# Token rows summed inside the gathering DMAs, into six accumulators, instead of on VectorE

## The chip, the cores and the metric

The kernel runs on one core of one Trainium2 chip. The metric is the device time of one execution in microseconds (us). The times before are 7422.84, 7378.67 and 7359.8 us in three runs, with a median of 7378.67 us. Engines are named as in the profile: PE is TensorE, DVE is VectorE, ACT is ScalarE, POOL is GpSimd and SP is SyncE.

## The reference, cut to what matters

A recommendation model scores 16384 examples. Each example averages 32 rows of a word table (50000 x 300, fp32), averages 20 rows of each of three 64-wide tables, looks up one row in each of four small tables, and sends the 748 numbers through three dense layers. A "wide" sum of scalars is added before the sigmoid.

```python
tok = word_emb[token_idx].mean(axis=1)          # 16384 x 32 rows of 300
e1 = emb_mh1[mh1_idx].mean(axis=1)              # e2, e3 alike; o1..o4 are one row each
emb = jnp.concatenate([tok, e1, e2, e3, o1, o2, o3, o4], axis=1)
h = jax.nn.relu(emb @ W1 + b1)                  # 748 -> 1024, then 512, then 256
...
return jax.nn.sigmoid(h @ Wd + bd + wide)
```

The change concerns `tok` alone: how the 32 rows of an example are fetched and added up.

## The kernel before, in words

The batch is cut into 128 tiles of 128 examples, one example per partition, and four tiles make a block of 512 for the dense layers. For each tile there are four kinds of work.

**Tokens** (`tokens`, L180). Eight groups of four indirect DMAs, issued from POOL (L186), each fetch one 1200-byte row for each of the 128 examples into a quarter of a tile `tok_rows` of 4 x 300 fp32. `tok_rows` has three buffers. DVE then adds the four rows of the group (L194: 600 elements, L197 or L199: 300) and adds them to the example's row `g` (L200). `g` also holds the sums of the small tables and is what the dense layers read.

**Counts** (`one_hots` L255, `counts` L273 and L280). The lookups in the small tables become matrix products. DVE compares the keys of six rows with an iota into two one-hot tiles, `row` and `slice`, which have two buffers. PE multiplies them into a PSUM tile `pc`, twelve matmuls in two groups of six, and ACT evicts each group into `cnt` (L280). A tile takes eleven such steps (`STEPS`), 22 evictions.

**Sums** (`small_sums`, L298 and L305). PE multiplies the counts of the tile before by the tables held in SBUF (138 matmuls `pg`), and DVE reduces the result into `g`.

**Dense layers** (`transposed` L340 and L341, `layer` L348 and L357, `mlp`). They run for the block of four tiles before, in fp32, spread over the steps of the next four tiles.

The order of every engine's queue is the order in which the Python loop at L411 to L445 emits the instructions. There is no scheduler. In step `i` of a tile it emits: the one-hots of step `i+1`, the count matmuls and evictions of step `i`, one portion of the tokens, one portion of the sums, and one portion of the dense layers. `Paced` doles out the portions: the token generator is advanced eight times over the eleven steps, at steps 0, 1, 2, 4, 5, 6, 8 and 9. So a group's three DVE additions stand in DVE's queue between the one-hots of two steps. A fresh buffer of `tok_rows` is free when the additions of the group three earlier are done. POOL does nothing else in the loop but issue these gathers, 32 for each tile.

The semaphores behind the gathers are eight lanes taken in turn, so a gather also waits for the gather eight places before it.

Of the kernel before, what the change touches and what calls it, by code (L numbers as in the profile page):

```python
# [8 lines left out]
F32 = mybir.dt.float32  # L9
# [3 lines left out]
U32 = mybir.dt.uint32  # L13
AF = mybir.ActivationFunctionType
ALU = mybir.AluOpType
AX = mybir.AxisListType

P = 128
N_TOK, TOK_D = 32, 300
N_MH, EMB = 20, 64  # L20
ROW = EMB + 1
D1, D2, D3 = 1024, 512, 256
TOK_GROUP = 4
BLOCK = 512
HALF = P // 2
N_SMALL = 3 * N_MH + 4
ONEHOT = 6
STEPS = -(-HALF // ONEHOT)
LULL = 12
# [14 lines left out]
def kernel(  # L44
# [21 lines left out]
    nc = tc.nc  # L66
    B = out.shape[0]
    NSUB = BLOCK // P
    M1, M2, M3 = D1 // P, D2 // P, D3 // P
# [3 lines left out]
    slices, n_h = {}, 0  # L73
    for f in SMALL:
        n = -(-tables[f].shape[0] // P)
# [5 lines left out]
    idxp = ctx.enter_context(tc.tile_pool(name="idx", bufs=2))  # L81
    keyp = ctx.enter_context(tc.tile_pool(name="keys", bufs=1))
    scp = ctx.enter_context(tc.tile_pool(name="sc", bufs=2))
    tokp = ctx.enter_context(tc.tile_pool(name="tok", bufs=3))
    ohp = ctx.enter_context(tc.tile_pool(name="onehot", bufs=2))
    cp = ctx.enter_context(tc.tile_pool(name="counts", bufs=2))
    gp = ctx.enter_context(tc.tile_pool(name="g", bufs=NSUB + 1))
    wp = ctx.enter_context(tc.tile_pool(name="wide", bufs=2 * NSUB))
    xp = ctx.enter_context(tc.tile_pool(name="x", bufs=1))
    op = ctx.enter_context(tc.tile_pool(name="o", bufs=1))  # L90
    ps_h = ctx.enter_context(tc.tile_pool(name="ps_h", bufs=2, space=bass.MemoryType.PSUM))
    ps_c = ctx.enter_context(tc.tile_pool(name="ps_c", bufs=2, space=bass.MemoryType.PSUM))
    ps_g = ctx.enter_context(tc.tile_pool(name="ps_g", bufs=2, space=bass.MemoryType.PSUM))
# [83 lines left out]
    bd_sb = const.tile([1, 1], F32, name="bd_sb")  # L177
    nc.scalar.dma_start(out=bd_sb, in_=bd)

    def tokens(g, it):  # L180

        for q in range(N_TOK // TOK_GROUP):
            rows = tokp.tile([P, TOK_GROUP * TOK_D], F32, name="tok_rows")
            for t in range(TOK_GROUP):
                j = q * TOK_GROUP + t
                nc.gpsimd.indirect_dma_start(  # L186
                    out=rows[:, t * TOK_D : (t + 1) * TOK_D],
                    out_offset=None,
                    in_=word,
                    in_offset=bass.IndirectOffsetOnAxis(ap=it[:, j : j + 1], axis=0),  # L190
                )
            n = TOK_GROUP * TOK_D // 2
            while n > TOK_D:
                nc.vector.tensor_add(rows[:, 0:n], rows[:, 0:n], rows[:, n : 2 * n])  # L194
                n //= 2
            if q == 0:
                nc.vector.tensor_add(g[:, 0:n], rows[:, 0:n], rows[:, n : 2 * n])  # L197
            else:
                nc.vector.tensor_add(rows[:, 0:n], rows[:, 0:n], rows[:, n : 2 * n])  # L199
                nc.vector.tensor_add(g[:, 0:n], g[:, 0:n], rows[:, 0:n])  # L200
            yield 1

    def load_indices(blk):


        b0 = blk * BLOCK
        it = idxp.tile([P, NSUB, N_TOK], I32, name="it")
        nc.sync.dma_start(
            out=it, in_=idx[b0 : b0 + BLOCK, 0:N_TOK].rearrange("(s p) c -> p s c", p=P)
        )  # L210
        ix = keyp.tile([P, NSUB // 2, 2, N_SMALL], I32, name="ix")
        for s in range(NSUB):
            nc.sync.dma_start(
                out=ix[(s % 2) * HALF : (s % 2 + 1) * HALF, s // 2],
                in_=idx[b0 + s * P : b0 + (s + 1) * P, IDX_MH:IDX_COLS].rearrange(
                    "(f p) c -> p f c", p=HALF
                ),
            )
        return it, ix
# [68 lines left out]
    def small_sums(g, cnt):  # L288


        by_slice = cnt.rearrange("l f p h -> l (f p) h")
        for i in (0, 2, 6, 4):
            pair = SMALL[i : i + 2]
            pg = ps_g.tile([P, 2, 3 * ROW], F32, name="pg")
            for j, f in enumerate(pair):
                h0, h1 = slices[f]
                for h in range(h0, h1):
                    nc.tensor.matmul(  # L298
                        pg[:, j, :], by_slice[:, :, h], terms[:, h, :], start=(h == h0), stop=(h == h1 - 1)
                    )  # L300
                    if h < h1 - 1:
                        yield 1
            at = TOK_D + i * ROW
            n = len(pair)
            nc.vector.tensor_reduce(  # L305
                g[:, at : at + n * ROW].rearrange("p (f d) -> p f d", f=n),
                pg[:, 0:n, :].rearrange("p f (c d) -> p f d c", c=3),
                AX.X,
                ALU.add,
            )  # L310
            yield n if i != 6 else n + LULL
# [32 lines left out]
    def layer(dst, weights, bias, src, kks, n_out):  # L344
        for m in range(n_out):
            ph = ps_h.tile([P, BLOCK], F32, name="ph", tag="ph")
            for k, kk in enumerate(kks):
                nc.tensor.matmul(  # L348
                    ph,
                    weights[:kk, k, m * P : (m + 1) * P],  # L350
                    src[:kk, k, :],
                    start=(k == 0),
                    stop=(k == len(kks) - 1),
                )
                if k < len(kks) - 1:
                    yield 1
            nc.scalar.activation(dst[:, m, :], ph, AF.Relu, bias=bias[:, m : m + 1])  # L357
            yield 1

    def mlp(blk, x, wides):  # L360

        h1 = xp.tile([P, M1, BLOCK], F32, name="h1", tag="odd")
        yield from layer(h1, w1_sb, b1_sb, x, chunk_k, M1)
        h2 = xp.tile([P, M2, BLOCK], F32, name="h2", tag="even")
        yield from layer(h2, w2_sb, b2_sb, h1, [P] * M1, M2)
        h3 = xp.tile([P, M3, BLOCK], F32, name="h3", tag="odd")
        yield from layer(h3, w3_sb, b3_sb, h2, [P] * M2, M3)
        po = ps_h.tile([1, BLOCK], F32, name="po", tag="ph")
        for k in range(M3):
            nc.tensor.matmul(po, wd_sb[:, k : k + 1], h3[:, k, :], start=(k == 0), stop=False)  # L370
        for s, wide in enumerate(wides):
            nc.tensor.matmul(  # L372
                po[:, s * P : (s + 1) * P], wide, ident, start=False, stop=(s == NSUB - 1)
            )
        y = op.tile([1, BLOCK], F32, name="y")
        nc.scalar.activation(y, po, AF.Sigmoid, bias=bd_sb)
        nc.sync.dma_start(
            out=out[blk * BLOCK : (blk + 1) * BLOCK, :].rearrange("n o -> o n"), in_=y
        )
        yield M3  # L380
# [23 lines left out]
    tiles = B // P  # L404
    mlp_size = NK * M1 + M1 * M2 + M2 * M3 + M3
    ctx.enter_context(tc.manual_schedule())
    it, ix = load_indices(0)
    sc = lookup_keys(ix)
    hot = one_hots(sc, 0, 0)
    gs, wides, layers, before = [], [], None, None  # L410
    for t in range(tiles + 1):  # L411
        s = t % NSUB
        sums = None
        if before:
            sums = Paced(small_sums(*before), n_h + LULL, STEPS)
        if t < tiles:
            if s == 0 and t:
                it, sc = next_it, next_sc
            g = gp.tile([P, G_COLS], F32, name="g")
            cnt = cp.tile([P, 2, HALF, n_h], FP8, name="cnt", tag="counts")  # L420
            toks = Paced(tokens(g, it[:, s, :].bitcast(U32)), N_TOK // TOK_GROUP, STEPS)
        for i in range(STEPS):
            if t < tiles:
                hot_now = hot
                if s == 1 and i == 0 and t + NSUB < tiles:
                    next_it, ix = load_indices(t // NSUB + 1)
                if s == 2 and i == 0 and t + NSUB < tiles + 1:
                    next_sc = lookup_keys(ix)
                if i < STEPS - 1:
                    hot = one_hots(sc, s, i + 1)  # L430
                elif t + 1 < tiles:
                    hot = one_hots(next_sc if s == NSUB - 1 else sc, (s + 1) % NSUB, 0)
                counts(cnt, hot_now, i)
                toks.go()
            if sums:
                sums.go()
            if layers:
                layers.go()
        if before:
            sums.finish()  # L440
            gs.append(before[0])
            wides.append(wide_term(before[0]))
        before = (g, cnt) if t < tiles else None
        if len(gs) == NSUB:
            if layers:  # L445
                layers.finish()
            layers = Paced(mlp(t // NSUB - 1, transposed(gs), wides), mlp_size, NSUB * STEPS)
            gs, wides = [], []
# [40 lines left out]
```

## Time and profile before

| What | Value |
|---|---|
| median of three runs | 7378.67 us |
| the profiled execution, its own time | 7632.91 us |
| its span, first to last instruction | 7631.1 us |
| mean granted TensorE clock | 0.874 |
| PE busy | 5876.7 us, 77% |
| DVE busy | 3534.9 us, 46% |
| ACT busy | 2659.7 us, 35% |
| POOL busy | 4052.0 us, 53% |
| gathers (L186) | 4096, 989 ns each |
| gather queue q0 | 629.41 MB, 30.0% of the time of 16 DMA engines |

Busy time is what an engine's instructions cover. A matmul's end is modelled, so PE's busy time says what PE was given, not when the results were there. A gather's POOL time is the time of issuing it; its data lands later. The profiled execution takes 254 us more than the median of the runs, so what is summed from the profile is compared with the profile's own time and then scaled.

### The profile page before, as it was taken

To read this page: it belongs to the slowest core of one execution; us is meant where nothing else is said; L and a number is where in the kernel's file an instruction comes from. 1 tells how busy PE (TensorE), PEld (TensorE's weight loads), DVE (VectorE), ACT (ScalarE), POOL (GpSimd) and SP (SyncE) were. 2 spreads that over 40 slices of the span, in tenths; PEclk is the share of its full clock that TensorE was granted. 3 is DMA by queue.
4 is the path that set the end of the run, shared out by engine and by line. 5 is a ranking of instruction groups with operands and counts; after the bars stand their busy time and mean duration, and the time that the engine had idled before them with its cause. 6 is when DMAs were issued, how large, how long until landed. Compare 5 with 4: busy or idle time off the path is not lost.

```text
span 7631.1 us, 100300 instructions
## 1 busy us (share of the span) xinstructions
PE 5876.7 (77%) x40960; PEld 3502.6 (46%) x40960; DVE 3534.9 (46%) x6977; ACT 2659.7 (35%) x3383; POOL 4052.0 (53%) x4103
## 2 busy tenths in 40 slices
PE   2677877877777777787778788787777777777779
PEld 2444444444444444444444444444444444444444
DVE  4544444444444444454444444444444444444442
ACT  4333333333333333333333333333333333333332
POOL 5555555555555555555555555555555555555551
PEclk8788888888888888888888888888888889888889
DMA  4333333333333333333333333333233333333330
GB/s 133 91 87 87 85 90 83 88 83 88 84 84 86 86 85 86 85 83 89 87 85 88 82 89 85 89 86 86 82 86 87 83 83 88 85 86 88 84 85 26
DMA packets 242810, 652.35 MB, mean 85 GB/s; under 512 B 105631, under 2 KB 109471, under 8 KB 242347
## 3 DMA queue, kind: packets, MB, share of 16 engines
q0 software_dynamic: 196608, 629.41, 30.0%
q1 hardware_dynamic: 42738, 10.83, 0.7%
q8 instruction: 320, 5.24, 0.3%
q10 hardware_dynamic: 3001, 5.69, 0.2%
q14 instruction: 143, 1.17, 0.0%
HBM read 645.59 MB, written 0.07 MB: 85 GB/s over the span
## 4 chain that ended last, share of the span: by engine, by line
PE 51%; another core or an unknown queue 23%; ACT 10%; issue 9%; DVE 4%; POOL 3%; DMA 0%; DVEq 0%; SPq 0%; ACTq 0%; POOLq 0%
PE ph L348 22%; PE pg L298 18%; PE pc L273 9%; ACT cnt L280 8%; POOL tok_rows L186 3%; ACT h L357 2%; PE pt L340 1%; DVE x L341 1%; DVE g L305 1%; PE po L370 1%; DVE slice L255 0%; DVE tok_rows L194 0%; PE po L372 0%; DVE tok_rows L199 0%
## 5 line engine op out<-in xcount | busy, mean ns | idle before, releaser
L186 POOL DMA_INDIRECT tok_rows<-in_word_emb_dram,it x4096 | 4051.1, 989 | 3442.7 <-DVE g L200 1363.5
L280 ACT ACTIVATE cnt<-pc 128x828 fp8e3<-128x828 f32 (+1 forms) x2816 | 2235.8, 840 | 3547.7 <-remote 1763.9
L298 PE MATMUL pg<-terms,cnt 128*128 128x195 bf16 x17664 | 2166.4, 274 | 350.9 <-issue 255.2
L255 DVE TENSOR_TENSOR row<-iota,sc 128x768 bf16<-128x768 bf16 (+1 forms) x1408 | 763.5, 542 | 2947.3 <-remote 1625.3
L298 PEld LDWEIGHTS <-cnt 128*128 128x128 fp8e3 x17664 | 1783.4, 147 | 602.7 <-issue 463.6
L273 PE MATMUL pc<-slice,row 64*128 64x138 bf16 x16384 | 874.2, 233 | 1219.9 <-ACT cnt L280 909.0
L273 PEld LDWEIGHTS <-row 64*128 64x128 bf16 x16384 | 566.3, 98 | 2343.3 <-issue 1831.2
L348 PE MATMUL ph<-x,w_sb 128*128 128x512 f32 (+1 forms) x3072 | 1605.6, 650 | 20.4 <-issue 19.9
L348 PE MATMUL ph<-h,w_sb 128*128 128x512 f32 x2560 | 1366.8, 660 | 21.4 <-issue 20.4
L348 PEld LDWEIGHTS ph<-x,w_sb 128*128 128x128 f32 (+1 forms) x3072 | 588.4, 211 | 489.6 <-issue 480.4
L255 DVE TENSOR_TENSOR slice<-iota,sc 128x828 bf16<-128x828 bf16 (+1 forms) x1408 | 805.0, 572 | 0.0
L194 DVE TENSOR_TENSOR tok_rows<-tok_rows 128x600 f32<-128x600 f32 x1024 | 793.7, 775 | 4.9 <-DMA tok_rows<-in_word_emb_dram,it 4.9
L357 ACT ACTIVATE h<-ph,b_sb 128x512 f32<-128x512 f32 x448 | 308.2, 688 | 1220.0 <-remote 507.5
L348 PEld LDWEIGHTS ph<-h,w_sb 128*128 128x128 f32 x2560 | 494.6, 214 | 410.1 <-issue 409.7
L305 DVE TENSOR_REDUCE g<-pg 128x130 f32<-128x390 f32 (+1 forms) x512 | 250.9, 508 | 836.5 <-remote 396.0
L199 DVE TENSOR_TENSOR tok_rows<-tok_rows 128x300 f32<-128x300 f32 x896 | 423.7, 473 | 30.8
L200 DVE TENSOR_TENSOR g<-g,tok_rows 128x300 f32<-128x300 f32 x896 | 421.8, 471 | 30.7
L341 DVE TENSOR_SCALAR x<-pt,scale 128x512 f32<-128x512 f32 (+1 forms) x192 | 139.0, 748 | 103.7 <-PE pt L340 77.7
L340 PE MATMUL pt<-ident,g 128*128 128x128 f32 (+1 forms) x768 | 126.6, 299 | 59.7 <-DVE x L341 59.7
L340 PEld LDWEIGHTS pt<-ident,g 128*128 128x128 f32 (+1 forms) x768 | 87.2, 147 | 98.8 <-DVE x L341 90.0
L280 ACT ACT_TABLE_LOAD x31 | 39.8, 1283 | 137.8 <-PE pc L273 137.7
L238 PE MATMUL pk<-ident_bf,keys 128*128 128x128 bf16 x128 | 22.5, 245 | 75.7 <-DVE keys L234 41.4
(35 smaller groups left out, 463.5 us busy)
## 6 DMA issues: line engine op xcount, KB each, us to landing
tok_rows<-in_word_emb_dram,it POOLq DMA_INDIRECT x4096
ix<-in_idx_dram SPq DMA_DIRECT2D x128, 32.0 KB
w_sb<-in_W_dram ACTq DMA_DIRECT2D x6, 512.0 KB
w_sb<-in_W_dram ACTq DMA_DIRECT2D x1, 2048.0 KB
it<-in_idx_dram SPq DMA_DIRECT2D x32, 64.0 KB
out_dram<-y SPq DMA_DIRECT2D x32, 2.0 KB
raw<-in_mh_dram SPq DMA_DIRECT2D x1, 422.5 KB
w_sb<-in_W_dram ACTq DMA_DIRECT2D x1, 256.0 KB
```

What stands on the lines that cost most here:

```text
L186: nc.gpsimd.indirect_dma_start(out=rows[:, t * TOK_D : (t + 1) * TOK_D], out_offset=None, in_=word, in_offset=bass.IndirectOffsetOnAxis(ap ...
L194: nc.vector.tensor_add(rows[:, 0:n], rows[:, 0:n], rows[:, n : 2 * n])
L199: nc.vector.tensor_add(rows[:, 0:n], rows[:, 0:n], rows[:, n : 2 * n])
L200: nc.vector.tensor_add(g[:, 0:n], g[:, 0:n], rows[:, 0:n])
L255: nc.vector.tensor_tensor(one[:, 0:rows, :].rearrange("p i (n d) -> p i n d", d=2), iota[:, 0:n].rearrange("p (n d) -> p n d", d=2).unsque ...
L273: nc.tensor.matmul(pc[:, f, k * n_h : (k + 1) * n_h], hot[0][half, k0 + k, :], hot[1][half, k0 + k, :], start=True, stop=True,)
L280: nc.scalar.activation(cnt[:, :, b + k0 : b + k0 + n, :].rearrange("l f k h -> l f (k h)"), pc[:, :, 0 : n * n_h], AF.Copy, scale=0.5, sat ...
L298: nc.tensor.matmul(pg[:, j, :], by_slice[:, :, h], terms[:, h, :], start=(h == h0), stop=(h == h1 - 1))
L305: nc.vector.tensor_reduce(g[:, at : at + n * ROW].rearrange("p (f d) -> p f d", f=n), pg[:, 0:n, :].rearrange("p f (c d) -> p f d c", c=3) ...
L340: nc.tensor.transpose(pt[:kk, s * P : (s + 1) * P], chunk(g, k), ident)
L348: nc.tensor.matmul(ph, weights[:kk, k, m * P : (m + 1) * P], src[:kk, k, :], start=(k == 0), stop=(k == len(kks) - 1),)
L357: nc.scalar.activation(dst[:, m, :], ph, AF.Relu, bias=bias[:, m : m + 1])
```

## The change

It does three things.

1. `gather` replaces the DMA half of `tokens`. At the start of a tile it emits all 32 gathers in POOL's queue. The target is one tile `tok_acc` of six rows of 300 fp32, with two buffers. The first six gathers overwrite an accumulator each; the other 26 carry `compute_op=ALU.add`, so that the DMA adds the fetched row to what the accumulator holds. Gather `j` adds to accumulator `j % 6` and, by the listing of the built instructions, waits for gather `j-6`.
2. The DVE half becomes three additions per tile, of 900, 300 and 300 elements, emitted after the eleven steps of the *next* tile, just ahead of that tile's `wide_term`. The first of them waits for the last gathers of its six accumulators. DVE's queue shrinks from 6864 to 4304 listed rows; PE's and ACT's have as many rows as before.
3. The output pool `op` goes away; the sigmoid's row `y` is kept in a third row of `h3`.

The tile of gathers `t` can start when the additions of tile `t-2` are done, which stand at the end of tile `t-1`'s steps.

```diff
+TOK_ACC = 6
-    tokp = ctx.enter_context(tc.tile_pool(name="tok", bufs=3))
+    tokp = ctx.enter_context(tc.tile_pool(name="tok", bufs=2))
-    op = ctx.enter_context(tc.tile_pool(name="o", bufs=1))
-    def tokens(g, it):
...
+    def gather(it):
+        acc = tokp.tile([P, TOK_ACC * TOK_D], F32, name="tok_acc")
+        for j in range(N_TOK):
+            a = j % TOK_ACC
+            nc.gpsimd.indirect_dma_start(
+                out=acc[:, a * TOK_D : (a + 1) * TOK_D],
+                out_offset=None,
+                in_=word,
+                in_offset=bass.IndirectOffsetOnAxis(ap=it[:, j : j + 1], axis=0),
+                compute_op=ALU.bypass if j < TOK_ACC else ALU.add,
+            )
+        return acc
+    def tokens(g, acc):
+        n = TOK_D
+        nc.vector.tensor_add(acc[:, 0 : 3 * n], acc[:, 0 : 3 * n], acc[:, 3 * n : 6 * n])
+        nc.vector.tensor_add(acc[:, 0:n], acc[:, 0:n], acc[:, n : 2 * n])
+        nc.vector.tensor_add(g[:, 0:n], acc[:, 0:n], acc[:, 2 * n : 3 * n])
...
-        h3 = xp.tile([P, M3, BLOCK], F32, name="h3", tag="odd")
+        h3 = xp.tile([P, M3 + 1, BLOCK], F32, name="h3", tag="odd")
...
-        y = op.tile([1, BLOCK], F32, name="y")
+        y = h3[0:1, M3, :]
...
-            toks = Paced(tokens(g, it[:, s, :].bitcast(U32)), N_TOK // TOK_GROUP, STEPS)
+            acc = gather(it[:, s, :].bitcast(U32))
...
-                toks.go()
...
             sums.finish()
+            tokens(before[0], before[2])
             gs.append(before[0])
             wides.append(wide_term(before[0]))
-        before = (g, cnt) if t < tiles else None
+        before = (g, cnt, acc) if t < tiles else None
```

More of the change, by code (lines that the diff above doesn't have):

```diff
@@ L178 @@
     nc.scalar.dma_start(out=bd_sb, in_=bd)
-    def tokens(g, it):
[L182 to L201, printed above, removed]
+    def gather(it):
[15 more added lines that the diff above has]
+        nc.vector.tensor_add(g[:, 0:n], acc[:, 0:n], acc[:, 2 * n : 3 * n])
     def load_indices(blk):
@@ L414 @@
         if before:
-            sums = Paced(small_sums(*before), n_h + LULL, STEPS)
+            sums = Paced(small_sums(*before[:2]), n_h + LULL, STEPS)
         if t < tiles:
```

## The prediction

> **What bounds the kernel now.** I read the page's groups first, then the waits by engine, then equal stretches of the run with and without dense layers, and last the timeline of one stall.
>
> ```profile
> span 7631.1 us, 100300 instructions
> ...
> PE 5876.7 (77%) x40960; PEld 3502.6 (46%) x40960; DVE 3534.9 (46%) x6977; ACT 2659.7 (35%) x3383; POOL 4052.0 (53%) x4103
> ...
> L186 POOL DMA_INDIRECT tok_rows<-in_word_emb_dram,it x4096 | 4051.1, 989 | 3442.7 <-DVE g L200 1363.5
> ```
>
> PE is at 77%, so the first guess is a PE bound. POOL's waits show how it spends a tile:
>
> ```profile
> POOL tok_rows L186 <- DVE g L200: 1363.5, 338, 8.0
> POOL tok_rows L186 <- issue: 1099.4, 3566, 1.6
> POOL tok_rows L186 <- DVE g L197: 911.1, 118, 16.2
> ```
>
> A gather costs 989 ns plus 0.27 us of issue (1099.4 us over 4096), 1.26 us in all, so 32 gathers keep POOL for 40.2 us a tile. For the other 18 us it waits until DVE's additions free a buffer. The stretches by stage come next: two of tiles that have counts and sums but no dense layers, then one that has them.
>
> ```profile
> core 0: us, PE busy (x) PEld busy (x) DVE busy (x) ACT busy (x) POOL busy (x), PEclk, DMA share, GB/s
> 96.00:156.00 60.00, 26.32 (x272) 21.30 (x270) 26.87 (x57) 17.41 (x22) 36.41 (x37) 0.73 0.35 95
> 212.00:264.00 52.00, 28.60 (x266) 22.48 (x266) 25.42 (x52) 17.33 (x23) 30.09 (x30) 0.64 0.33 90
> 318.00:374.00 56.00, 45.95 (x338) 26.48 (x333) 27.91 (x59) 19.57 (x25) 32.73 (x33) 0.88 0.35 94
> ```
>
> Each stretch is about one tile. PE's work rises from 26 to 46 us and the tile stays near 56. From the trace, by the first count matmul of each tile, tiles 1 to 3 took 60.2, 56.6 and 52.0 us and the later ones 58.5 on average. So PE's own work does not set the tile. A step that runs freely takes 3.5 us, and eleven of them with 2 us of transposes and output products make 40.5 us; 18 us of each tile are stalls. The timeline shows what a stall looks like:
>
> ```profile
> 179.38 0.36 PE L273 MATMUL pc<-slice,row 64*128 64x138 bf16 x6 [1.71 <-issue]
> 179.67 0.89 PEld L298 LDWEIGHTS <-cnt 128*128 128x128 fp8e3 x10
> 180.76 0.47 DVE L200 TENSOR_TENSOR g<-g,tok_rows 128x300 f32<-128x300 f32 x1
> 183.16 0.95 POOL L186 DMA_INDIRECT tok_rows<-in_word_emb_dram,it  x1 [0.30 <-issue]
> ...
> 186.91 0.95 POOL L186 DMA_INDIRECT tok_rows<-in_word_emb_dram,it  x1 [0.30 <-issue]
> 188.48 0.87 ACT L280 ACTIVATE cnt<-pc 128x828 fp8e3<-128x828 f32 x1 [9.15 <-remote]
> 189.40 0.53 PE L273 MATMUL pc<-slice,row 64*128 64x138 bf16 x6 [6.32 <-ACT cnt L280]
> 189.94 0.56 DVE L255 TENSOR_TENSOR row<-iota,sc 128x768 bf16<-128x768 bf16 x1 [8.70 <-PE pc L273]
> ```
>
> The count matmuls were given to PE by 179.5, yet ACT could evict them only from 188.48. Nothing runs from 183 to 188 but POOL's gathers. The release comes when the run of gathers has ended (187.86) and its last data can have landed. I counted evictions over the whole trace by where they fall in a run of gathers (pauses over 1 us end a run), from 264 us on:
>
> - first 6 us of a run: 0.450 a us (19.5 us a tile);
> - the rest of a run: 0.189 a us (21.0 us a tile);
> - the 2.2 us after a run: 0.448 a us (7.0 us a tile);
> - the rest of the pause: 0.553 a us (11.1 us a tile). Free speed is two per 3.5 us, 0.57.
>
> So what shows is that **PE's results come late once gathers have run for 6 us, and recover when they pause**. I infer that the gathers do this; the page shows only that both go together. Runs end by themselves at 4, 8 or 12 gathers, since three buffers hold twelve.
>
> **What the Trainium skill says.** "DMA: Bandwidth & Descriptors", section "SWDGE vs HWDGE vs iDMA": accumulation in a DMA is available only from GpSimd's queue, so all 32 gathers stay on POOL. The same page, "Rules for kernel authors": an accumulating DMA reads its destination and writes it later, so an earlier one on the same bytes must be waited for; the listing of the changed kernel has that wait, on gather j-6. No run here shows its price yet. "SBUF — State Buffer", section "Who interferes with whom": DMA never contends with a compute engine. The counts above do not fit that as they stand, and I go by the counts. "TensorE: Matmul & The Clock Gate", Part 1: the array clock halves when the array is little used. The trace agrees in direction: 0.64 to 0.73 without dense layers, 0.88 with.
>
> **The change part by part**, for one tile.
>
> 1. *DVE's additions.* Removed: L194 793.7, L197 60.2, L199 423.7, L200 421.8, in all 1699.4 us, 13.3 us a tile. Added: 300 elements take 0.47 and 600 take 0.775, so 900 take about 1.08; with two of 0.47, 2.0 us. DVE falls from 27.6 to 16.3 us of work. On the path this gives little: DVE's own idle stands before `row`, waiting for PE, so the additions lay beside other work. I take nothing for it. If that cover is false, the most is 11.3 us a tile. The new 2.0 us stand in one piece between two tiles, ahead of `wide` and, once in four tiles, of the transposes; the first one-hot of the next tile is already emitted. Under 1 us, taken as nothing beside the pause they shorten.
> 2. *POOL's waits on buffers.* The 18 us of waiting on L200 and L197 go, and 32 gathers follow each other for 40.2 us. What is late next is the next tile's first gather, which waits for the additions at the end of the tile. So POOL works 40.2 us and then pauses once, instead of pausing three to four times.
> 3. *The price of an adding gather.* Not in the trace. Issue: at least the 1.26 us of a plain gather. "Collectives: The Full Stack", section "The bandwidth ceiling", says that an adding transfer needs two reads, hence two read descriptors; if issue doubles with them, 2 x 0.989 + 0.27 = 2.25 us for 26 of 32, a run of 66 us. Engine time: 30.0% of 7631 us over 4096 gathers is 0.56 us; doubled, 1.12, still under 1.26, so hidden. A gain isn't excluded by a rule, but nothing is left out of the work. I take 1.26 us for both, since the fixed part of an issue and the writes do not double.
> 4. *The wait for gather j-6.* Six issues later is 7.5 us. In the trace plain data landed 2.5 us after issue began (3017.12 to 3019.6). Even with 0.56 us more it is hidden. It decides nothing below 7.5 us of landing; with L us the run is 32/6 x L.
> 5. *`y` in `h3`, SP's output DMA:* the same instructions; nothing. The buffer of `h3` is next written by a later block's `h1`, a tile or more after the 2 KB have left.
>
> *Sum.* During the run of 40.2 us: 6 x 0.450 + 34.2 x 0.189 = 9.2 of the 22 evictions. In the 2.2 us after: 1.0. The remaining 11.8 at 0.553: 21.4 us. The tile takes 40.2 + 2.2 + 21.4 = 63.8 us against 58.5. Times 128, plus 143 us ahead of and behind the tiles (7631 - 128 x 58.5), 8309 us of profile. Scaled by 7378.67 / 7632.91 to the median of runs: 8032, rounded 8030 us.
>
> **The rivals.**
>
> *Relief, on the other side.* Gathers and PE do not hinder each other; the stalls came of POOL, DVE and PE waiting in a ring over three buffers, and the change cuts the ring. Then a tile is the larger of POOL's 40.2 and PE's 40.5, the latter 46.3 at the clock of 0.874: 46.3 x 128 + 143 = 6069, scaled 5870 us. For it: POOL's 18 us of waiting on DVE. Against it: 183 to 188 us above, where additions are done and data landed. It decides once a long run lets over 0.30 evictions a us through: then 2.7 + 10.3 + 1.0 leave 8.0, or 14.5 us, and the tile is 57, under today's.
>
> *No change.* Each gather costs PE a fixed amount, 18 us / 32 = 0.56 us, however they are spaced. There are as many gathers, so 40.5 + 18 = 58.5 us: 7300 to 7450. Against it: the first 6 us of a run are nearly free.
>
> *A slow adding gather.* Issue at 2.25 us, or landing at 12 us or more, makes the run itself 64 to 66 us, with PE hindered all along: 66 + 2.2 us at the least, and 81 if the rate stays 0.189. That is 8580 to 10160; I put it at 9300. Against it: the engine time is small beside 1.26.
>
> *Full stop.* Long runs let nothing through after 6 us, since a little used array also loses clock: 2.7 + 1.0 leave 18.3, 33.1 us, a tile of 75.5 and 9480 us. It is the upper end of my own case; a rate of 0.25 gives 60.1 us and 7570 us, the lower.
>
> **How the numbers follow.** Hindered PE with cheap adds, 8030 us (own range 7570 to 9480): 0.50. Slow adding gather: 0.16. No change: 0.07. Part relief, 6600 to 7300: 0.08. Full relief, 5600 to 6600: 0.19. A measurement of this kernel tells about 1% from no change, so faster has 0.27, the same 0.07, slower 0.66. The range of 6300 to 9700 leaves out most of full relief (0.13) and the end of the slow adds (0.06); cases of both signs are in it, and the first one's own range stands above.
>
> **What would show it.** Step 1: DVE near 2090 us busy in all. Steps 2 and 3: DMA_INDIRECT near 989 ns, runs of 32 gathers, one pause a tile, and its releaser the new last addition. Step 4: hardly any POOL wait on a DMA. The sum: evictions crowded into the pause, `cnt <- remote` waits longer than 10 us, and a granted clock under 0.874. I am wrong if PE's steps stay near 3.5 us while POOL runs, or if DMA_INDIRECT or the waits on gathers grow past 7.5 us.

## The result, and the profile after

The changed kernel took 7469.68 us (median of four runs, 7468.09 to 7470.38) beside 7369.24 us for the kernel before on the same chip. The ratio is 1.012, 95% interval 1.0078 to 1.0163: slower by 1.2%, where 8.8% had been forecast. The profiled execution took 7469.2 us, so its sums need no scaling.

The page of the changed kernel, the lines that answer to those of before, with the gather queue and the chain by engine:

```profile
span 7467.4 us, 96178 instructions
...
PE 5355.6 (72%) x40960; PEld 3285.7 (44%) x40960; DVE 2201.3 (29%) x4417; ACT 2632.5 (35%) x3383; POOL 6089.4 (82%) x4103
...
q0 software_dynamic: 516096, 629.41, 59.9%
...
POOL 78%; issue 20%; PE 1%; DMA 0%; ACT 0%; DVE 0%; SPq 0%; POOLq 0%; DVEq 0%; ACTq 0%
...
L186 POOL DMA_INDIRECT tok_acc<-in_word_emb_dram,it x4096 | 6088.5, 1486 | 1284.8 <-issue 1247.2
```

A gather now costs 1486 ns on average where it was 989, POOL's share rose from 53% to 82%, and the chain that ended last lies on POOL. Its waits, and the two that stand behind it (us in total, times, longest):

```profile
POOL tok_acc L186 <- issue: 1247.2, 4095, 0.3
...
DVE tok_acc L198 <- DMA tok_acc<-in_word_emb_dram,it: 2076.5, 128, 43.0
...
PE pc L272 <- DVE slice L254: 984.7, 67, 35.3
```

POOL waits for nobody: 0.3 us of issue between two gathers, never more. VectorE's first addition (L198) waits for the tile's last gathers, up to 43 us, and TensorE waits for VectorE, which stands in that queue. Three stretches of one tile each, the first two without dense layers, as in the view of before:

```profile
core 0: us, PE busy (x) PEld busy (x) DVE busy (x) ACT busy (x) POOL busy (x), PEclk, DMA share, GB/s
102.80:160.40 57.60, 23.39 (x297) 19.83 (x297) 17.54 (x38) 18.86 (x24) 47.88 (x32) 0.71 0.60 86
218.40:275.80 57.40, 19.28 (x242) 16.35 (x242) 15.18 (x31) 15.65 (x20) 47.70 (x32) 0.65 0.61 86
333.50:390.80 57.30, 45.16 (x347) 27.77 (x347) 17.76 (x38) 22.32 (x29) 47.59 (x32) 0.89 0.62 87
```

As before, the tile doesn't follow PE's work; now it is exactly POOL's 32 gathers. In the trace (medians by place in the tile) the first six gathers, which overwrite, take 0.95 to 1.13 us and come 1.25 to 1.43 us apart, but for the third with 1.64 and 1.95 us; the 26 that add take 1.55 us and come 1.85 us apart. 32 gathers keep POOL for 57.3 us. 128 times that, plus 39 us ahead of the first gather and 93 us behind the last, is the span of 7467 us within rounding.

What TensorE does while POOL runs is the other half of the result. The timeline in the middle of a tile (start, length, engine, line):

```profile
3611.40 0.54 PE L272 MATMUL pc<-slice,row 64*128 64x138 bf16 x12
3611.80 1.61 ACT L279 ACTIVATE cnt<-pc 128x828 fp8e3<-128x828 f32 x2 [1.89 <-PE pc L272]
...
3612.17 1.79 POOL L186 DMA_INDIRECT tok_acc<-in_word_emb_dram,it  x1 [0.30 <-issue]
...
3614.99 0.54 PE L272 MATMUL pc<-slice,row 64*128 64x138 bf16 x12
3615.38 1.61 ACT L279 ACTIVATE cnt<-pc 128x828 fp8e3<-128x828 f32 x2 [1.97 <-PE pc L272]
```

Steps begin 3.6 us apart and their counts are evicted 0.4 us after the first matmul, in a run of gathers that has lasted since the start of the kernel. Before, 90% of the evictions began within 6.9 us of the start of their last matmul; now 90% begin within 0.96 us. The forecast stall is not there.

One thing is needed to read the experiments: the kernel before is not equally fast on every chip. It took 5613.36 us on the chip of the first round below (the fast chip in what follows) and 7626.72, 7348.64, 7670.40 and 7373.02 us on those of the next four (slow chips). No chip was used in two of these rounds, so "chip" stands for the chip together with whatever else differs from round to round.

### The profile page after: what moved, and what is told of

The parts are those of the page before. It is cut to its first block, busy times and chain, and to the rows that moved or that the text cites. A ratio compares the mean times of both kernels' runs of the same rounds, so it can differ in the third digit from the quotient of the medians.

```text
span 7467.4 us, 96178 instructions
## 1 busy us (share of the span) xinstructions
PE 5355.6 (72%) x40960; PEld 3285.7 (44%) x40960; DVE 2201.3 (29%) x4417; ACT 2632.5 (35%) x3383; POOL 6089.4 (82%) x4103
## 3 DMA queue, kind: packets, MB, share of 16 engines
q0 software_dynamic: 516096, 629.41, 59.9%
## 4 chain that ended last, share of the span: by engine, by line
POOL 78%; issue 20%; PE 1%; DMA 0%; ACT 0%; DVE 0%; SPq 0%; POOLq 0%; DVEq 0%; ACTq 0%
POOL tok_acc L186 78%; PE ph L347 1%; DMA raw<-in_mh_dram 0%; PE pt L339 0%; ACT raw L152 0%; DMA tok_acc<-in_word_emb_dram,it 0%; ACT terms L155 0%; SPq L149 0%; DMA it<-in_idx_dram 0%; POOLq L484 0%; PE po L369 0%; DVE raw L157 0%; ACT L152 0%; DVE tok_acc L198 0%; PE po L371 0%
## 5 line engine op out<-in xcount | busy, mean ns | idle before, releaser
L186 POOL DMA_INDIRECT tok_acc<-in_word_emb_dram,it x4096 | 6088.5, 1486 | 1284.8 <-issue 1247.2
L297 PE MATMUL pg<-terms,cnt 128*128 128x195 bf16 x17664 | 1936.3, 262 | 0.4
L297 PEld LDWEIGHTS <-cnt 128*128 128x128 fp8e3 x17664 | 1659.7, 145 | 175.8 <-issue 28.3
L272 PE MATMUL pc<-slice,row 64*128 64x138 bf16 x16384 | 791.5, 230 | 1005.6 <-DVE slice L254 984.7
L347 PE MATMUL ph<-x,w_sb 128*128 128x512 f32 (+1 forms) x3072 | 1472.6, 605 | 0.0
L347 PE MATMUL ph<-h,w_sb 128*128 128x512 f32 x2560 | 1268.6, 621 | 0.0
L198 DVE TENSOR_TENSOR tok_acc<-tok_acc 128x900 f32<-128x900 f32 x128 | 140.3, 1096 | 2076.5 <-DMA tok_acc<-in_word_emb_dram,it 2076.5
L347 PEld LDWEIGHTS ph<-x,w_sb 128*128 128x128 f32 (+1 forms) x3072 | 538.4, 194 | 403.4 <-issue 402.3
L339 PE MATMUL pt<-ident,g 128*128 128x128 f32 (+1 forms) x768 | 184.2, 398 | 655.1 <-DVE g L200 534.3
L199 DVE TENSOR_TENSOR tok_acc<-tok_acc 128x300 f32<-128x300 f32 x128 | 60.3, 471 | 4.4
```

Of the source, the lines that this page charges most:

```text
L186: nc.gpsimd.indirect_dma_start(out=acc[:, a * TOK_D : (a + 1) * TOK_D], out_offset=None, in_=word, in_offset=bass.IndirectOffsetOnAxis(ap= ...
L198: nc.vector.tensor_add(acc[:, 0 : 3 * n], acc[:, 0 : 3 * n], acc[:, 3 * n : 6 * n])
L199: nc.vector.tensor_add(acc[:, 0:n], acc[:, 0:n], acc[:, n : 2 * n])
L272: nc.tensor.matmul(pc[:, f, k * n_h : (k + 1) * n_h], hot[0][half, k0 + k, :], hot[1][half, k0 + k, :], start=True, stop=True,)
L297: nc.tensor.matmul(pg[:, j, :], by_slice[:, :, h], terms[:, h, :], start=(h == h0), stop=(h == h1 - 1))
L339: nc.tensor.transpose(pt[:kk, s * P : (s + 1) * P], chunk(g, k), ident)
```

## The experiments

Each ratio is against the kernel before on the same chip. "Results late" is the time from the start of the last count matmul of a bank to the start of its eviction, worked out from the trace, given as what 90% stay within.

### Round 1: gathers without adding, on a chip where the kernel before is fast

**All gathers plain.**

```diff
-                compute_op=ALU.bypass if j < TOK_ACC else ALU.add,
+                compute_op=ALU.bypass,
```

> The changed kernel with all 32 gathers of a tile plain (each overwrites its accumulator, so 26 rows of each sum are lost); queues, waits and buffers as in the changed kernel. Theory A (plain gathers that follow each other for over 6 us hinder PE): POOL back at 1.26 us a gather, a tile of about 64 us, 7900 to 8100 us. Theory B (gathers do not hinder PE; the kernel before lost its time in the ring of POOL, DVE and PE over three buffers, and the changed kernel is bound by POOL at 1.79 us a gather): a tile of 41 to 47 us, 5500 to 6200 us.

Measured: 5491.47 us, ratio 0.9799 (0.9767 to 0.983); results late by 0.96 us.

```profile
PE 5155.1 (94%) x40960; PEld 3144.9 (57%) x40960; DVE 2193.2 (40%) x4417; ACT 2628.9 (48%) x3383; POOL 4112.1 (75%) x4103
...
L186 POOL DMA_INDIRECT tok_acc<-in_word_emb_dram,it x4096 | 4111.2, 1004 | 1284.7 <-issue 1237.7
```

POOL runs without a pause here too, at 1.25 us a gather in the median and 1.31 on average, and PE is busy 94% of the span. On this chip no late results show, though plain gathers follow each other all along. This looked like the end of the prediction's theory; in round 3 the same kernel behaves otherwise.

**No additions on VectorE** (one per tile is left, of the first group).

```diff
-            n = TOK_GROUP * TOK_D // 2
-            while n > TOK_D:
-                nc.vector.tensor_add(rows[:, 0:n], rows[:, 0:n], rows[:, n : 2 * n])
-                n //= 2
             if q == 0:
-                nc.vector.tensor_add(g[:, 0:n], rows[:, 0:n], rows[:, n : 2 * n])
-            else:
-                nc.vector.tensor_add(rows[:, 0:n], rows[:, 0:n], rows[:, n : 2 * n])
-                nc.vector.tensor_add(g[:, 0:n], g[:, 0:n], rows[:, 0:n])
+                nc.vector.tensor_add(g[:, 0:TOK_D], rows[:, 0:TOK_D], rows[:, TOK_D : 2 * TOK_D])
```

> The kernel before with seven of the eight groups of token rows not added at all (one addition per tile is left, to write g), so that POOL waits for DVE once a tile; gathers plain as before, in three buffers. Theory A: the stalls stay, 7200 to 8100 us. Theory B: the ring is cut, 5500 to 6200 us.

Measured: 7595.61 us, ratio 1.3541 (1.3502 to 1.3581), with less work. The waits say why:

```profile
DVE g L193 <- DMA tok_rows<-in_word_emb_dram,it: 2713.6, 127, 29.2
POOL tok_rows L186 <- DMA tok_rows<-in_word_emb_dram,it: 2416.0, 861, 4.4
```

With nobody reading the rows, POOL waits before nearly every group, 2.8 us on average, until gathers have landed: 8 x (4 x 1.25 + 2.5) = 60 us a tile, beside 58.3 us in the trace. The edit put a new wait in the place of the additions, so it says nothing about what they cost. Results were not late (0.96 us): that the time falls into theory A's range is chance.

**Additions put back beside plain gathers**, as idle ones on a zero tile, paced over the steps.

```diff
-                compute_op=ALU.bypass if j < TOK_ACC else ALU.add,
+                compute_op=ALU.bypass,
...
+        for q in range(N_TOK // 4):
+            n = 2 * TOK_D
+            nc.vector.tensor_add(spare[:, 0:n], spare[:, 0:n], spare[:, 0:n])
+            n = TOK_D
+            nc.vector.tensor_add(spare[:, 0:n], spare[:, 0:n], spare[:, n : 2 * n])
+            if q:
+                nc.vector.tensor_add(g[:, 0:n], g[:, 0:n] if q > 1 else spare[:, n : 2 * n], spare[:, 0:n])
+            yield 1
```

> As e1_plain, with the token additions of the kernel before put back in DVE's queue at the same eight steps (22 of them, 13 us a tile), on a spare tile of zeros that no gather writes, so with their load and without their waits. Theory A: about as e1_plain, 7900 to 8100 us. Theory B: within 3% of e1_plain, under 6300 us. Theory C (DVE's work inside the steps is what slows them): back at 7200 to 7400 us.

Measured: 5663.13 us, ratio 1.0092 (1.0062 to 1.0122); 3.1% over the run without them. DMA_INDIRECT rose from 1004 to 1045 ns and the mean distance of gathers from 1.31 to 1.35 us; 32 x 0.042 us x 128 tiles is the whole difference of 172 us. So VectorE's additions cost little, just over the 3% that theory B allowed, and what they cost comes through POOL. Theory C falls.

**No gathers**, all additions kept, on zero tiles.

```diff
-            rows = tokp.tile([P, TOK_GROUP * TOK_D], F32, name="tok_rows")
-            for t in range(TOK_GROUP):
...
+            rows = still[q % 3]
```

> The kernel before with the gathers left out: all additions stay where they are and add three tiles of zeros. It measures PE, ACT and DVE without POOL. Theories A and B: 5500 to 6100 us, 41 to 46 us a tile. Theory C: 7200 us or more.

Measured: 5237.18 us, ratio 0.9336 (0.9309 to 0.9363), or 40.9 us for each of 128 tiles with all that lies around them: the floor without gathers, and under the 5500 to 6100 us that were expected. The prediction had 40.5 us for PE's own work.

### Round 2: on a chip where the kernel before is slow

**The kernel before and the changed kernel, unchanged.**

> The kernel before, unchanged, profiled beside the other kernels of this round. Theory P (placement: the kernel before has two behaviours, one with results of TensorE arriving late, 7370 us, and one without, 5613 us): if it runs near 5613 us here, its trace shows TensorE busy over 90% of the span, few waits put down to an unknown queue, and DMA_INDIRECT still near 989 ns each. Theory Q (the gathers themselves are dearer in one of the two): DMA_INDIRECT is then well away from 989 ns, or queue 0's share per gather is well away from 0.56 us of an engine.

Measured: 7634.62 us, as the kernel before itself (7626.72); results late by 6.9 us; DMA_INDIRECT 987 ns and q0 at 30.5% of the span, as in the trace of before. Both theories were written for a run near 5613 us, which did not come: this is the slow behaviour once more, and no trace shows the kernel before on the fast chip. What can be compared between the kinds of chip is the kernel with all gathers plain: 1004 ns a gather in round 1 and 971 ns in round 3. The price of issuing a gather is thus no part of the difference; that speaks against theory Q.

> The changed kernel, unchanged, beside the kernel before on one chip. Theory P2 (it is bound by POOL's issue, 32 gathers of 1.79 us on average a tile, 57.3 us, and so does not care what slows the kernel before): 7440 to 7500 us again, ratio 1.32 to 1.34 if the kernel before takes 5613 us. Rival R2 (both kernels suffer from the same disturbance, so the ratio stays near 1.01): 5600 to 5800 us.

Measured: 7470.37 us, ratio 0.9802 (0.9747 to 0.9857). It is the time of the first comparison, 7469.68, to 0.01%, while the kernel before stands 3.5% higher. Whether the change looks like a loss of 1.2% or a gain of 2.0% depends on the kernel before.

**13 adding gathers a tile, in one block at its end.**

```diff
-                compute_op=ALU.bypass if j < TOK_ACC else ALU.add,
+                compute_op=ALU.bypass if j < N_TOK - 13 else ALU.add,
```

> The changed kernel with 13 of a tile's 32 gathers adding instead of 26 (the other 13 overwrite their accumulator, so that their rows are left out of the sum). Theory P2 (an adding gather costs POOL a fixed 0.60 us more in issue): DMA_INDIRECT mean (19 x 0.95 + 13 x 1.55)/32 = 1.19 us, a tile 19 x 1.25 + 13 x 1.85 = 47.8 us, x 128 + 140 = 6260 us, POOL without a pause. Rival (the adding gathers slow each other down, through the DMA engines' work, so the price goes with how many there are in a row): the 13 that remain cost under 1.4 us or the plain ones over 1.05 us, and the time is away from 6260 us by over 150 us.

Measured: 8117.79 us, ratio 1.0646 (1.0586 to 1.0706): half of the dear gathers are gone and the kernel is 8.7% slower than with all of them. Both theories of this run missed: prices are as forecast (0.95 and 1.55 us), yet POOL pauses 14 us a tile, since TensorE is late. The timeline of one tile, in which the 19 plain gathers run from 3771.6 to 3796:

```profile
3781.09 0.54 PE L272 MATMUL pc<-slice,row 64*128 64x138 bf16 x12
...
3782.84 1.91 PE L347 MATMUL ph<-h,w_sb 128*128 128x512 f32 x4
...
3784.68 0.09 PEld L272 LDWEIGHTS <-row 64*128 64x128 bf16 x1 [0.76 <-issue]
3784.88 0.86 ACT L279 ACTIVATE cnt<-pc 128x828 fp8e3<-128x828 f32 x1 [4.96 <-remote]
...
3788.43 0.86 ACT L279 ACTIVATE cnt<-pc 128x828 fp8e3<-128x828 f32 x1 [2.69 <-remote]
...
3791.96 0.14 PEld L297 LDWEIGHTS <-cnt 128*128 128x128 fp8e3 x1 [1.21 <-issue]
3791.96 0.38 PE L297 MATMUL pg<-terms,cnt 128*128 128x195 bf16 x1 [0.37 <-issue]
...
3793.36 0.38 PE L297 MATMUL pg<-terms,cnt 128*128 128x195 bf16 x1 [1.02 <-issue]
...
3794.79 0.32 PE L297 MATMUL pg<-terms,cnt 128*128 128x195 bf16 x1 [1.05 <-issue]
```

From 3791 on TensorE is not stopped by any data that the profile shows: it waits for "issue" and begins a matmul every 1.4 us, with one weight load between them, where 13 to 15 such pairs take 1.4 us when it runs freely. This document calls that crawling. The late results come before it: the twelve count matmuls began by 3781.41, and sums and dense matmuls followed at full pace until 3784.2, yet their two banks were evicted only at 3784.88 and 3788.43. In this trace 598 evictions begin over 3 us after the start of their last matmul, and TensorE begins 46 further instructions (median) in that time. So the results fall behind first and the pace of the beginnings drops later. Whether the work or the signal of its end is late can't be told, as a matmul's end is modelled. Counted over the whole trace, TensorE instructions (matmuls and weight loads) begun per us, by the gather that POOL is issuing (0 to 31; the fourth and fifth rows are later runs, the last is the first run of round 1; at even pace neighbouring gathers differ too, so single cells say little):

```
gather                      5     8    12    16    20    24    28
kernel before            17.2  19.4  15.3  13.2   5.2   9.6  13.0
changed kernel           10.8  13.6  11.9  10.6  12.3  13.6   0.7 (waits for L198)
13 adding, at the end    18.7   8.8   3.2   1.6   1.6   8.0  11.3
13 adding, alternating   10.4  17.9  20.2  15.8  11.9  12.3   9.1
all plain, slow chip     17.4   9.3   2.0   4.2   2.8   0.7   0.9
all plain, fast chip     10.4  17.6  14.1  20.1  11.5  21.2  11.0
```

In the run with 13 adding gathers at the end the pace falls after some eight plain gathers and recovers a few gathers after the adding ones have begun (number 19).

**Pairs of rows in seven buffers**, all additions kept.

```diff
-TOK_GROUP = 4
+TOK_GROUP = 2
-    tokp = ctx.enter_context(tc.tile_pool(name="tok", bufs=3))
+    tokp = ctx.enter_context(tc.tile_pool(name="tok", bufs=7))
```

> The kernel before with the same additions on VectorE, but groups of two rows in 7 buffers (14 rows in flight instead of 12, freed two at a time), y in h3 as in the changed kernel. Theory D (the kernel before loses time where gathers wait for VectorE to free a whole group): 5480 to 5600 us, a ratio of 0.975 to 0.998, POOL's waits for VectorE down from 18 us a tile to under 8. Rival (POOL's waits cost nothing, what the kernel before loses is TensorE's own, and 32 short additions load VectorE more than 24): 5610 to 5750 us.

Measured: 7347.93 us, ratio 0.9641 (0.9587 to 0.9695). The expectation was written for the fast chip, so its times do not apply; POOL still waits 16.5 us a tile for VectorE (1728.4 + 387.4 us), and results are late by 7.0 us. Finer buffers don't cure it.

### Round 3: order and distance of the gathers

From here the theory is: on these chips plain gathers that follow each other closely hold TensorE's results and make it crawl, and adding gathers do not.

**Groups of eight rows, four plain and then four adding**, nothing left out of the sum.

```diff
-TOK_GROUP = 4
+TOK_GROUP = 8
+TOK_ACC = 4
-                    out=rows[:, t * TOK_D : (t + 1) * TOK_D],
+                    out=rows[:, t % TOK_ACC * TOK_D : (t % TOK_ACC + 1) * TOK_D],
+                    compute_op=ALU.bypass if t < TOK_ACC else ALU.add,
```

> The kernel before with groups of eight rows in the same four-row buffers: rows 0 to 3 of a group plain, rows 4 to 7 added into them by the DMAs, and one set of VectorE's additions for eight rows instead of four. Nothing is left out. Theory H (TensorE's results are held only once plain gathers have followed each other for more than about 6 us, and adding gathers hold nothing): plain runs last 5.0 us here, results are not held, POOL sets the time with 16 x 1.25 + 16 x 1.86 = 49.8 us a tile, 6370 + 140 = about 6500 us (6300 to 6800), and the matrix steps run near 3.5 us. Rival M (it is the mixture that does harm, as in the run with 13 adding gathers, 8118 us): 7600 us or more. On a chip that does not hold results, 6500 us as well.

Measured: 6972.06 us, ratio 0.948 (0.9431 to 0.953); results late by 1.1 us. No crawl, as theory H says; but 7% over its time. DMA_INDIRECT was 1356 ns instead of 1250: the first adding gather of a group took 1.79 us and the plain ones up to 1.26. Why was not followed.

**The 13 adding gathers alternating with plain ones.**

```diff
-                compute_op=ALU.bypass if j < N_TOK - 13 else ALU.add,
+                compute_op=ALU.bypass if j < TOK_ACC or j % 2 else ALU.add,
```

> As the run with 13 adding gathers a tile, and as many plain ones, 19, but from the seventh gather on adding and plain ones take turns (the plain ones overwrite, so that their rows are left out of the sum). Theory H: no run of plain gathers is longer than the six at the start of a tile, results are not held, POOL's 19 x 1.25 + 13 x 1.86 = 47.9 us a tile decide: 6130 + 140 = about 6280 us (6150 to 6600) where the other order took 8118 us. Rival M (the mixture, or the average rate of gathers, decides, not the order): within 4% of 8118 us.

Measured: 6508.23 us, ratio 0.885 (0.8803 to 0.8896), against 8117.79 (1.0646) in the other order, on another chip of the slow kind; results late by 1.1 us instead of 9.0. The same gathers, in another order: the mixture is not the cause.

**All plain, with a memset of POOL after each.**

```diff
-                compute_op=ALU.bypass if j < TOK_ACC else ALU.add,
+                compute_op=ALU.bypass,
             )
+            nc.gpsimd.memset(spare, 0.0)
```

> All 32 gathers of a tile plain (rows beyond six left out of the sum), each followed by a memset of 128 x 384 on POOL, so that the gathers come at about the adding gathers' distance, 1.75 to 1.9 us instead of 1.25. Theory T (the rate: plain gathers hold TensorE's results because they come 1.25 us apart): on a chip where the kernel before takes 7370 us or more, results come within 1.2 us, and POOL's 56 to 61 us a tile set 7300 to 7900 us. Theory K (the kind: a plain gather holds results at any distance): results come up to 20 us late and the time is 8100 us or more.

**All plain, again**, with the edit of the first run of round 1.

> The changed kernel with all gathers plain, again (5491 us on a chip where the kernel before took 5613 us). If the holding of results belongs to the chip and the kernel before takes 7370 us or more here: results are held through the whole of a tile's 32 plain gathers, 40.2 us of POOL and then the work of TensorE that was held, 8500 us or more. If it belongs to the kernel before's own order: 5400 to 5700 us again.

Measured, one time each: 6746.81 us spaced and 9428.48 us unspaced, where the kernel before takes 7348.64. First the spaced run: POOL's groups and ACT's largest wait; then the unspaced run's largest wait of ACT, which is put down to "remote", a release that the profile ties to no instruction:

```profile
L189 POOL DMA_INDIRECT tok_acc<-in_word_emb_dram,it x4096 | 4158.8, 1015 | 715.6 <-issue 678.3
...
L196 POOL MEMSET spare<- 128x384 f32 x4096 | 1785.1, 436 | 2.4
...
ACT cnt L283 <- PE pc L276: 2650.0, 1135, 36.0
```

```profile
ACT cnt L279 <- remote: 3924.0, 374, 33.5
```

The gathers are the same, 4096 of 1015 and of 971 ns. Spaced, they come 1.55 us apart and results are late by 0.96 us; at 1.25 us by 15.2 us, the longest wait 33.5 us. So theory K falls, and theory T's forecast for the results holds; its 7300 to 7900 us were missed, since the gathers came closer than the 1.75 to 1.9 us it assumed. Whether the distance counts or another instruction in between is the question of round 4. And the chip counts: the very kernel that took 5491 us in round 1 takes 9428 us here.

### Round 4: where the threshold lies, with all additions kept

The kernel before (`y` in `h3` for room) with a memset after each gather, of 128 or 256 elements; the third run has pairs of rows in six buffers, the fourth two memsets of 384 after every fourth gather.

```diff
                     in_offset=bass.IndirectOffsetOnAxis(ap=it[:, j : j + 1], axis=0),
                 )
+                nc.gpsimd.memset(spare, 0.0)
```

> The kernel before, all additions kept, with a memset of 128 x 128 on POOL after each plain gather (y in h3, to make room). Gathers then come about 1.0 + 0.2 + 0.15 = 1.35 us apart, 43 us a tile, against TensorE's 40.9. Theory T (it is the rate that holds TensorE's results; at 1.61 us apart nothing was held, at 1.25 everything): if the threshold lies below 1.35, 5700 to 6000 us where the kernel before takes 7350 to 7630; if above, 6900 to 7600. Theory L (it is the length of a run of plain gathers without any other instruction of POOL between them): 5700 to 6000 us whatever the distance.

> The same with a memset of 128 x 256 after each gather: about 1.47 us apart, 47 us a tile. Theory T with the threshold below 1.47 us, and theory L: 6050 to 6350 us. Theory T with the threshold above: 6800 to 7600 us.

> Groups of two rows in 6 buffers (the same 12 rows in flight), with a memset of 128 x 128 after each gather. Where results are not held: 5700 to 5900 us, as with groups of four or up to 2% less, since buffers come free two at a time; where they are held at 1.35 us apart: 6800 to 7400 us.

> The kernel before with two memsets of 128 x 384 (0.44 us each) after every fourth gather: four gathers 1.25 us apart, then a pause of about 1 us, 1.5 us a gather on average, 48 us a tile. Theory T with a backlog that drains in the pause (what counts is the average rate over some 6 us): 6150 to 6450 us. Rival (four gathers 1.25 us apart are already enough, a pause of 1 us does not undo it): 6900 to 7700 us.

Measured, with the median distance of gathers from the trace:

| run | distance, us | results late, us | time, us | ratio (95%) |
|---|---|---|---|---|
| memset 128 | 1.34 | 7.0 | 7270.49 | 0.9485 (0.9433 to 0.9537) |
| pairs, memset 128 | 1.34 | 6.8 | 7229.24 | 0.9408 (0.9376 to 0.944) |
| memset 256 | 1.44 | 4.2 | 6529.63 | 0.8494 (0.8464 to 0.8524) |
| pause after four | 1.25 to 1.5, then 2.2 to 2.4 | 1.5 | 6689.19 | 0.8712 (0.8684 to 0.874) |

At 1.34 us TensorE is held as at 1.25, at 1.44 partly, at 1.55 (round 3) not. Theory L falls: another instruction between gathers is not enough. A pause of about 1 us after four close gathers serves nearly as well as distance, so a limit on the rate over some 6 us, near 1.5 us a gather, would describe all of these runs; it is a description, not a mechanism. The pause after four missed its 6150 to 6450 us by 4% and its rival's 6900 too: its gathers came 1.59 us apart on average and not 1.5, which makes 50.9 us a tile on POOL. The memset of 256 missed its 6050 to 6350 us by 3%. Its results are still late by 4.2 us, and its chain has 4% of time whose end the profile puts down to no known instruction:

```profile
POOL 52%; PE 21%; issue 11%; DVE 6%; another core or an unknown queue 4%; ACT 3%; DMA 2%; POOLq 0%; DVEq 0%; SPq 0%; ACTq 0%
```

POOL leads the chain, where the kernel before had PE with 51% and an unknown queue with 23%.

### Round 5: the best version, and the changed kernel again

Pairs of rows in six buffers, a memset of 256 after each gather.

> Groups of two rows in 6 buffers with a memset of 128 x 256 after each plain gather, all additions kept: 1.45 to 1.5 us a gather, 46 to 48 us a tile on POOL. Theory T: results come at most 4 us late at this distance, as in the run with groups of four at the same distance (6530 us), so 6250 to 6550 us where the kernel before takes over 7300; the finer buffers save at most the 1.5 us a tile that POOL waited for VectorE there. Rival (with POOL's pauses for buffers gone, nothing breaks the runs and results are held again): 6800 us or more.

Measured: 6367.74 us, ratio 0.8631 (0.8586 to 0.8676); distance 1.44 us, results late by 3.4 us; POOL waits for hardly anything but issue:

```profile
DVE tok_rows L201 <- DMA tok_rows<-in_word_emb_dram,it: 1782.1, 1311, 4.4
...
POOL tok_rows L187 <- issue: 669.1, 3901, 1.3
```

It beats the kernel before by 13.7% and the changed one by 14.7% on a chip of the slow kind. It was not run on the fast one. There the kernel before needs 42.7 us a tile ((5613 - 143) / 128), and 32 gathers at this run's mean distance of 1.51 us need 48.4 us: by that estimate it would lose there.

> The changed kernel on one more draw of a chip, beside the kernel before. It is bound by POOL's issue: 7460 to 7480 us whatever the chip, while the kernel before has shown 5613 us on one chip and 7349 to 7670 us on others. A time away from 7470 us by over 1% would mean that the issue of adding gathers differs from chip to chip.

Measured: 7468.84 us, ratio 1.012 (1.0067 to 1.0172). Three rounds give 7469.68, 7470.37 and 7468.84 us, beside 7369, 7627 and 7373 for the kernel before: the changed kernel's time is POOL's, the same wherever it was run. It was not run on the fast chip either. If it takes 7470 us there too, it is 33% slower than the kernel before, by estimate from 5613 us.

## Why the prediction was wrong, step by step

- **The step that failed** is the one under *Sum*: "During the run of 40.2 us: 6 x 0.450 + 34.2 x 0.189 = 9.2 of the 22 evictions". It carried the hindrance over from gathers that overwrite, 1.25 us apart, to gathers that add. These come 1.85 us apart, their results are late by 0.96 us, and TensorE begins 11 to 23 instructions a us among them (gathers 7 to 24 of a tile). The prediction's own test, PE's steps staying near 3.5 us while POOL runs, decided against it. Whether a gather that adds hinders less also at the same distance can't be told: none came closer than 1.84 us.
- **The hindrance itself was real.** With all gathers plain in the changed order, which is what the step assumed, the kernel takes 9428 us; the full stop had been put at 9480. *Relief*, that gathers and PE do not hinder each other, falls there, and is true on the chip of round 1. *No change* had nearly the right number for a reason that is wrong: a fixed cost to TensorE per gather cannot give 6747 us spaced and 9428 us unspaced.
- **Step 3, the price of adding**, was the other miss, of size: 1.26 us was taken and 1.85 measured, inside the bound of 2.25. The engine time was right in kind: 59.9% of 7467 us over 4096 gathers is 1.09 us, and by the packets of the adding gathers alone it is 1.19 us each, 6% over the bound of 1.12 and still hidden behind 1.85. The reason given, "the fixed part of an issue and the writes do not double", was wrong by 0.60 us of issue a gather; which part of the issue takes them is not shown.
- **Steps 1, 2, 4 and 5.** VectorE fell to 2201 us, near the 2090 forecast, and this gave nothing: it waits for gathers instead. The 18 us of POOL's waits went; but the pause that was to follow did not come, since POOL is never done early. The wait for gather j-6 is hidden: POOL shows waits on issue alone, and by its DMA packets an adding gather has landed 3.7 us after its issue began (median), where 7.5 were allowed. Nothing of the output's move is in the chain.
- **Where the gain went.** POOL's tile was 40.2 us of gathers and 18 of waiting. It is 57.3 us of gathers and no waiting: the change bought 18 us and paid 17.1 for it, 26 times 0.60 and some slower plain gathers. That alone would be a small gain on the 58.5 us a tile of the profile of before. On the chip of the comparison the kernel before takes (7369 - 143) / 128 = 56.5 us a tile, by estimate, and the 0.8 us more times 128 are the 100 us of loss. TensorE's relief is behind that and can't be seen. That 8030 was only 7.5% off is luck: the two misses had opposite signs; the combination, TensorE free and POOL the bound, was none of the cases, because *A slow adding gather* kept TensorE hindered.
- **What stays open.** Why plain gathers closer than about 1.5 us hold TensorE's results, and why not on the chip of round 1. The share of the DMA engines is not it: in the tile shown from the run with 13 adding gathers it is 0.47 from 3795.1 to 3800, where 5 matmuls begin, while in the alternating run it is 0.56 in a stretch of 22.2 us in which 175 begin. The granted clock is not it: 0.50 in that stretch and 1.00 from 3771.6 to 3779.1, a factor of 2 where the pace falls by more than 10. Nor is it a gather's own issue time, nor slower transfers: with all gathers plain a gather has landed 2.5 us after its issue began (median, from the DMA packets) on the fast chip and on the slow one. The packets of the instruction queue q8, 320 in each run and by their bytes 64 for each instruction of TensorE, take 1.03 us on average on the fast chip and 1.05 on the slow one, so nothing points to slower fetching. The section "Who interferes with whom" of "SBUF — State Buffer" in the Trainium skill says that DMA does not contend with compute engines; the crawl shows a dependence on the gathers, but no run shows that it lies in SBUF.

## What to carry to other kernels

An operation that moves work into a DMA is first priced on the queue that issues it: here 0.60 us more for each of 26 gathers a tile ate the 18 us that the change set free. A hindrance that is read from one kind of transfer holds for that kind at that distance only; count the slowed engine's instructions per us, by the transfer in flight, and change the distance before building a sum on it. And run the kernel before on more than one chip when its own trace shows a stall nobody can name: where the stall comes on one chip and not on another, the same change can look like a gain or a loss.

## What the runs showed that was not expected

- An adding gather of 128 rows of 1200 bytes costs POOL 1.55 us of issue against 0.95, its data packets are 1200 bytes instead of 4800 (144 packets a gather instead of 48, worked out from q0's 516096 and 196608; 16 of either are of 4 bytes), and it takes 1.19 us of DMA engine time against 0.57 for the plain ones beside it.
- TensorE can fall from about 15 to 1 or 2 instructions a us for 20 us and more, with "issue" as its wait, after its results have begun to come late, while plain gathers come 1.25 us apart; at 1.55 us apart it does not.
- The same kernel, all gathers plain, took 5491 us on one chip and 9428 on another, with gathers of 1004 and 971 ns.
- Slower issue was faster: a memset of 0.33 us after each gather took 15% off the kernel before on such a chip.
